# Sparse attention on one core: the attention stream starts one share sooner, and the second tile of an output pair may take the way over DRAM and be turned one product later

## The chip, the cores and the metric

The kernel runs on one core of one Trainium2 chip. The metric is device time in microseconds (us), the median of several executions. All arithmetic is fp32 except where stated.

## The reference

```python
# x: (2708, 1024); adj: (2708, 2708), 0/1, each entry is 1 with chance 0.0014771; W_*: (1024, 1024)
h = relu(layernorm(x))
q, k, v = h @ W_q.T + b_q, h @ W_k.T + b_k, h @ W_v.T + b_v
z = (q @ k.T) / sqrt(1024) * adj
z = where(z == 0, -10000, z)
out = x + relu(softmax(z, axis=1) @ v)
```

A row of adj has about four ones. Softmax over such a row is a sum over its few neighbours, so the kernel never forms the 2708 x 2708 scores.

## The kernel before

**Stages.** The kernel reads adj once, lists each row's neighbours, and sorts the rows by their number of neighbours into 21 full tiles of 128 rows (tiles 0 to 20) and a rest of 20 rows. Tile t has a fixed number K[t] of neighbour slots. W_q and W_k are multiplied into one matrix M, so that a score is a dot product of a row q = h M with a neighbour's row of h. The values are not formed per neighbour: the attention weights add up neighbours' rows of h into a row u, and only u is multiplied by W_v.

**TensorE: units.** The matrix products are written as 20 units (`units`), each of 256 rows, a pair of tiles, against a 1024 x 1024 matrix: units 0 to 9 make q from h (pairs (0,1), (2,3), ...), units 10 to 19 make the output from u. The output pairs are, in order, (6,5) (4,3) (2,0) (20,7) (13,17) (18,12) (19,11) (15,10) (14,1) (16,9); the 21st tile, 8, is left over (`alone`) and done singly at the end, its turned rows being `T_alone`. A unit is a Strassen-like scheme of seven products (`multiply`), each eight matmuls of 128x512, in the order s2, a12, s4, s3, then a11 and s1 of the next unit (`between`, `opened`), then a22. A `psy` row is a product by a matrix in wlow (the differences T), a `ps` row one by M.

**Operands.** A product needs its rows turned, with the 1024 columns across the partitions. `blocks` makes the operands of a pair: `upper` makes a11 and a12 from the pair's first tile, `lower` makes a22 and, by four additions, s1 to s4 from its second tile. While unit n runs, `after(i)` is called after its i-th product; the upper half of unit n+1 is written at i == 0 and the lower half at i == 2. A tile of u gets there in one of two ways:
- held in SBUF and turned by TensorE: eight transposes of 128x128 (L415) into two PSUM tiles pt, of which ScalarE copies one (L718) and VectorE reads the other in its additions (L722);
- faced: ScalarE copies u into v in another order (L944), a DMA of ScalarE's queue writes v to u_dram (L946), `load_rows` reads it back by quarters into `or` with four DMAs of SyncE's queue (L700), and VectorE turns it by two stream transposes (L705). In the four additions one becomes a subtraction in place.

`sums` decides at the end of a tile's sums: it is faced if that end falls, in program order, no later than product 2 of the unit two ahead of the one that uses it. `load_rows` of unit n+2 is called in unit n at i == 4; before it the stream is driven on until both tiles are done.

**Attention.** One Python generator, `attention`, goes over the tiles in the order 6, 5, 4, 3, 2, the second half of the hosts (SECOND), 0, 20, 7, 13, 17, 18, 12, 19, 11, 15, 10, 14, 1, 16, 9, 8. For a tile it gathers the rows of q (`fetch`, tile pq, L612) and the neighbours' rows of h into buffers g0 to g10 and two buffers in wlow (L610), both as indirect DMAs from POOL's queue. VectorE makes one dot product per slot (L863), ScalarE the exponentials (L872), VectorE the weights (L906 to L911), ScalarE the first term of u (L912), VectorE the other terms (L923). A buffer g goes back to the gathers when its sum is done. While a tile's sums run, the next tile's scores may run ahead of its weights. VectorE's order is the program's order, and all engines work through theirs in order. `advance(share)` lets the generator emit about three us of VectorE's work after each product, beginning in unit 5 (FIRST is 4); the share is 20.9/7 or, near the end, 21.5/7 us, less 2.3/7 for each faced tile of the next pair. VectorE's other work stands between these: the evictions of the products (L1130, the u2 of a unit's c12) and the operands.

Of the kernel before, what the change touches and what calls it, by code (L numbers as in the profile page):

```python
# [30 lines left out]
BARE = 20  # L31
# [34 lines left out]
def tile_preln_masked_attention(  # L66
# [109 lines left out]
    t = 0  # L176
    while t < NT:
# [4 lines left out]
        t = e  # L182
# [28 lines left out]
    def row_tile(name):  # L211
        return work.tile([P, D], FT, tag="row", name=name, bufs=ROWS)
# [402 lines left out]
    FIRST = EARLY // 2  # L615
# [187 lines left out]
    wanted, g_of, tq, first_q = [], {}, {}, []  # L803
# [11 lines left out]
    def ask(t):  # L815

        g_of[t] = []
        wanted.extend((t, s) for s in range(K[t]))

    def fetch(t):  # L820

        if t not in g_of:
            ask(t)
        if t == BARE:
            return
        assert formed.issuperset(range(EARLY) if t < EARLY or t == SECOND else (t,)), t
        tq[t] = work.tile([P, D], FT, tag="hT", name=f"pq_{t}", bufs=2)
        if t == SECOND:
            assert EARLY in formed
            gather(tq[t][:HP], q_dram[:, :], t, SLOTS - WIDE, HP)  # L830
            nc.gpsimd.dma_start(tq[t][HP:], q_late[:HP, :])
        elif t >= EARLY:
            nc.gpsimd.dma_start(tq[t], q_late[(t - EARLY) * P:(t - EARLY + 1) * P, :])
        else:
            got = gather(tq[t], q_dram[:, :], t, SLOTS, P)
            if t == order[0]:
                first_q.append(got)

    def fill():
        while wanted and free:  # L840
            t, s = wanted.pop(0)
            g = free.pop(0)
            if s == K[t]:
                half = slice(HOSTS.index(t) * HP, (HOSTS.index(t) + 1) * HP)
                nc.gpsimd.dma_start(g[:HP], v_dram[half, :])
            else:
                with tc.issue_after(first_q[0].ins) if first_q else nullcontext():
                    gathered.append(gather(g, h_dram[:, :], t, s, P, skip=True))
            g_of[t].append(g)

    def chained(step):

        with tc.issue_after(chain[-1].ins):
            chain.append(step())
# [64 lines left out]
    def sums(t):  # L919
        u, coef, m = us.pop(t)  # L920
        for s in range(0 if t in EMPTY else 1, K[t]):
            fill()
            chained(lambda: nc.vector.scalar_tensor_tensor(  # L923
                u, g_of[t][s], coef[:, s:s + 1], u, op0=ALU.mult, op1=ALU.add))
            free.append(g_of[t][s])
            yield 1.3
        fill()
        if t in HOSTS:
            chained(lambda: nc.vector.scalar_tensor_tensor(
                u[:HP], g_of[t][K[t]][:HP], m[:HP, 3:4], u[:HP], op0=ALU.mult, op1=ALU.add))  # L930
            free.append(g_of[t][K[t]])
            yield 1.3
            fill()
        g_of.pop(t)
        if t == SECOND:
            nc.sync.dma_start(v_dram, u)
            whole_second.append(True)
            return
        unit = next((n for n, pair in enumerate(units) if pair[0] == "o" and t in pair[1:]), len(units))
        if now <= [unit - 2, 2] or unit >= len(units) - 1:  # L940
            faced_tiles.add(t)
        if t in faced_tiles:
            v = row_tile(f"v_{t}")
            nc.scalar.copy(v.rearrange("p (a c r) -> p c a r", a=QUADS, r=QP),  # L944
                           u.rearrange("p (c a r) -> p c a r", a=QUADS, r=QP))
            nc.scalar.dma_start(u_dram[t * P:(t + 1) * P, :], v)  # L946
        elif near(t):
            held[t] = u
        else:
            nc.sync.dma_start(u_dram[t * P:(t + 1) * P, :], u)  # L950
        done.add(t)
# [7 lines left out]
    def attention(order):  # L959
        for t in order[:2]:  # L960
            ask(t)
        free.extend(slots)

        fetch(order[0])
        fill()
        yield 0.0
        marked(0, EARLY)
        yield 0.0
        after = order[1:] + [None, None]
        yield from scores(order[0], after[0])  # L970
        for i, t in enumerate(order):
            nxt = after[i]
            ahead = nxt is not None and K[t] + K[nxt] <= HIGH + 1
            part = scores(nxt, after[i + 1]) if nxt is not None else iter(())
            if ahead:

                for _ in range(min(2, K[nxt] - 1)):
                    yield next(part, 0.0)
            weights(t)
            yield 0.6  # L980
            if ahead:
                yield from part
            yield from sums(t)
            yield from part
# [4 lines left out]
    order = [6, 5, 4, 3, 2, 0, 20, 7, 13, 17, 18, 12, 19, 11, 15, 10, 14, 1, 16, 9, 8]  # L989
# [3 lines left out]
    spent, now = [0.0], [0, 0]  # L993
# [5 lines left out]
    def advance(us):  # L999

        spent[0] -= us
        while spent[0] < 0:
            step = next(stream, None)
            if step is None:
                break
            spent[0] += step
# [192 lines left out]
    o_pairs = [(order[i], order[i + 1]) for i in range(0, FULL - 1, 2)]  # L1199
    alone = order[-1]  # L1200
    units = [("q",) + p for p in q_pairs] + [("o",) + p for p in o_pairs]
# [29 lines left out]
        summed.append(True)  # L1231

    single = {}

    opened(0)
    for n, unit in enumerate(units):
# [6 lines left out]
        turn = n in (0, FIRST - 1)  # L1243
        share = (20.9 if n < len(units) - 5 else 21.5) / 7
        if n in (last_q, last_q + 1):
            share -= 2.3 / 7 * (n - last_q + 1)
        nxt = units[n + 1] if n + 1 < len(units) else None
# [4 lines left out]
        def after(i):  # L1252
# [43 lines left out]
                nc.vector.tensor_scalar(msq, msq, MLIMIT, None, op0=ALU.is_gt)  # L1296
            if n > FIRST:
                advance(share)
            if nxt is not None:

                if i == (3 if n == 0 else 4 if turn else 0):
                    ops_of[n + 1] = blocks(*rows_of[n + 1], nc.gpsimd if n + 1 < FIRST - 1 else None)
                    with tc.issue_after(products[-1].ins) if n + 1 == FIRST else nullcontext():
                        ops_of[n + 1][1]()
                if i == (4 if n == 0 else 5 if turn else 2):
                    ops_of[n + 1][2]()
                    rows_of.pop(n + 1)
                    if n == last_q - 1:
                        all_rows()
                if i == 3:  # L1310
                    banks_of[n + 1] = banks_for(bp_sb)
                if i == 6 and n + 2 < FIRST:
                    natural_rows(n + 2)
                if i == (2 if FIRST <= n <= last_q - 2 else 3 if n == last_q else 4) and n + 2 > FIRST and n + 2 < len(units) and n + 2 not in rows_of:
                    while units[n + 2][0] == "o" and not done.issuperset(units[n + 2][1:]):
                        advance(1.0)
                    rows_of[n + 2] = load_rows(units[n + 2])
# [259 lines left out]
```

## Time and profile before

| | |
|---|---|
| median of 3 runs | 627.59 us (627.45 to 627.91) |
| profiled execution | 628.18 us, its span 626.5 us |
| mean granted TensorE clock | 0.999 |
| TensorE busy | 619.6 us, 99% of the span |
| VectorE | 525.1 us, 84% |
| ScalarE | 291.1 us, 46% |
| GpSimd (POOL) | 366.2 us, 58% |
| DMA packets | 182.19 MB, mean 291 GB/s |

Times of single instructions are from the profiled execution, in us from the start of its span; its own time is 0.59 us above the median. PE is TensorE, PEld its weight loads, DVE VectorE, ACT ScalarE, SP SyncE. A row of a timeline has the start, the duration, the engine, the line of the kernel, the operation, what is written and read, and the shapes; a bracket at its end is the idle time of the engine just before, with what ended it. A row of grouped instructions has their count, then busy time and the mean in ns, then idle time ahead of them and what ended most of it.

### The profile page before, as it was taken

How to read it: one execution, taken by the hardware profiler on the slowest of the kernel's cores; microseconds unless marked ns; L12 is line 12 of the kernel's file. 1: busy time of each engine (PE TensorE's matmuls, PEld its weight loads, DVE VectorE, ACT ScalarE, POOL GpSimd, SP SyncE). 2: the span in 40 equal slices, each digit the busy share in tenths (PEclk: the TensorE clock that was granted, in tenths of full speed). 3: DMA queues.
4: the chain of work that ended last, by engine and by line, in shares of the span. 5: the costliest groups of instructions: out<-in, count | busy, mean ns of one | idle time of the engine just before them, and what ended most of it. 6: DMA issues, size and time to landing. Idle time of an engine off the chain costs nothing.

```text
span 626.5 us, 6070 instructions
## 1 busy us (share of the span) xinstructions
PE 619.6 (99%) x1579; PEld 310.9 (50%) x1579; DVE 525.1 (84%) x1022; ACT 291.1 (46%) x421; POOL 366.2 (58%) x394
## 2 busy tenths in 40 slices
PE   9999999999999999999999999999999999999996
PEld 5777767444444445454444444444444444444442
DVE  4999878987988845989897999998997998988741
ACT  3538985759677373344232433444342334342300
POOL 2648870786668477666543333778465776752241
PEclk9999999999999999999999999999999999999999
DMA  8999898688697559996687999999999999996481
GB/s 338 407 360 328 336 349 324 211 272 326 237 377 271 175 180 360 322 410 197 198 348 203 394 313 272 316 346 346 333 270 351 296 312 301 335 280 167 104 298 71
DMA packets 65088, 182.19 MB, mean 291 GB/s; under 512 B 9959, under 2 KB 20023, under 8 KB 64408
## 3 DMA queue, kind: packets, MB, share of 16 engines
q0 software_dynamic: 26656, 86.02, 43.3%
q1 hardware_dynamic: 31594, 71.53, 33.5%
q10 hardware_dynamic: 6798, 24.20, 9.8%
q8 instruction: 14, 0.23, 0.2%
q14 instruction: 26, 0.21, 0.1%
HBM read 146.70 MB, written 43.36 MB: 303 GB/s over the span
## 4 chain that ended last, share of the span: by engine, by line
PE 99%; POOL 0%; DVE 0%; POOLq 0%; issue 0%
PE ps L1010 46%; PE psy L1010 33%; PE ps_y L476 7%; PE ps_x L476 4%; PE ps_z L476 4%; PE pt L415 3%; PE ps_y L511 1%; PE ps_h L1229 0%; PE ps_v L594 0%; DVE y_alone L1393 0%; POOL out_dram L1377 0%; POOLq L1399 0%; POOL hsum L121 0%; PE ps_in L678 0%; PE ps_all L680 0%
## 5 line engine op out<-in xcount | busy, mean ns | idle before, releaser
L610 POOL DMA_INDIRECT g<-h_dram,tab x92 | 114.0, 1239 | 58.9 <-DVE u L923 18.5
L1010 PE MATMUL ps<-M,a 128*128 128x512 f32 x320 | 144.0, 593 | 0.0
L1010 PE MATMUL psy<-wlow,s 128*128 128x512 f32 x320 | 143.9, 592 | 0.0
L863 DVE SCALAR_TENSOR_TENSOR junk<-g,pq 128x1024 uint8<-128x1024 f32 x91 | 111.1, 1221 | 7.3 <-DMA g<-h_dram,tab 3.1
L1010 PE MATMUL ps<-M,s 128*128 128x512 f32 x240 | 107.9, 592 | 0.0
L1010 PEld LDWEIGHTS psy<-wlow,s 128*128 128x128 f32 x320 | 60.0, 190 | 72.1 <-issue 71.4
L1010 PEld LDWEIGHTS ps<-M,a 128*128 128x128 f32 x320 | 59.9, 190 | 71.8 <-issue 71.4
L923 DVE SCALAR_TENSOR_TENSOR u<-g,coef,u 128x1024 f32<-128x1024 f32 x68 | 87.1, 1281 | 3.9 <-ACT u L912 2.4
L389 DVE FIND_INDEX8 at<-ones,adj 128x8 uint32<-128x685 f32 (+1 forms) x88 | 74.5, 866 | 0.0
L1010 PEld LDWEIGHTS ps<-M,s 128*128 128x128 f32 x240 | 45.5, 190 | 57.2 <-issue 56.5
L1010 PE MATMUL psy<-wlow,a 128*128 128x512 f32 x160 | 71.9, 592 | 0.0
L368 ACT ACTIVATE sized<-adj 128x2708 uint8<-128x2708 f32 (+1 forms) x22 | 54.2, 2466 | 6.8 <-DMA adj<-in_adj_dram 5.5
L1114 POOL DMA_INDIRECT y<-in_x_dram,tab x19 | 35.3, 1856 | 32.2 <-ACT y L1131 18.9
L298 POOL TENSOR_TENSOR hsum<-hsum,x 128x256 f32<-128x256 f32 (+1 forms) x56 | 38.7, 734 | 26.1 <-DVE wlow L444 22.0
L1010 PEld LDWEIGHTS psy<-wlow,a 128*128 128x128 f32 x160 | 30.4, 190 | 38.3 <-issue 36.6
L808 POOL DMA_INDIRECT out_dram<-y,tab x21 | 25.8, 1229 | 21.7 <-issue 13.9
L1010 PE MATMUL ps<-wlow,s 128*128 128x512 f32 x80 | 36.0, 593 | 0.0
L944 ACT COPY v<-u 128x1024 f32<-128x1024 f32 x19 | 19.9, 1045 | 26.4 <-DVE u L923 23.1
L912 ACT ACTIVATE u<-g,coef 128x1024 f32<-128x1024 f32 x17 | 19.5, 1149 | 23.0 <-DVE coef L911 17.8
L626 POOL DMA_INDIRECT tab_dram<-tab,pos_i x22 | 21.6, 982 | 14.7 <-DVE pos_i L689 9.2
L760 ACT COPY ps<-bp_sb 128x512 f32<-128x512 f32 x42 | 24.5, 594 | 10.3 <-DVE y L1149 9.6
L276 ACT ACTIVATE x<-x,r 128x1024 f32<-128x1024 f32 (+1 forms) x22 | 25.8, 1232 | 6.3 <-POOL r L266 6.3
(253 smaller groups left out, 849.7 us busy)
## 6 DMA issues: line engine op xcount, KB each, us to landing
adj<-in_adj_dram SPq DMA_DIRECT2D x21, 1354.0 KB, 9.6
x<-in_x_dram SPq DMA_DIRECT2D x21, 512.0 KB, 4.3
h_dram<-x ACTq DMA_DIRECT2D x21, 512.0 KB, 8.0
u_dram<-v ACTq DMA_DIRECT2D x19, 512.0 KB, 6.7
or<-u_dram SPq DMA_DIRECT2D x76, 128.0 KB, 6.9
q_late<-q SPq DMA_DIRECT2D x12, 512.0 KB, 5.4
pq<-q_late POOLq DMA_DIRECT2D x12, 512.0 KB, 9.3
M<-in_wv_dram SPq DMA_DIRECT2D x3, 1024.0 KB, 10.1
```

Source lines behind the costliest of these rows:

```text
L276: nc.scalar.activation(xs[i][:n], xs[i][:n], AF.Relu, bias=r[:n, 4, i:i + 1], scale=r[:n, 3, i:i + 1])
L298: small.append(nc.gpsimd.tensor_add(hsum[:n, cols], hsum[:n, cols], xt[:n, cols]))
L368: nc.scalar.activation(sized[:n], a[:n, :, :PW], AF.Abs, accum_out=total[:n, t:t + 1])
L389: nc.vector.max_index(at[:n, k - first_k, g, :], ones[:n, 0:8], a[:n, g, :])
L476: mm = nc.tensor.matmul(bank, a_tile(o + H * a[0], a[1], i), b(o), start=first and o == 0, stop=(o == H - 1), skip_group_check=True)
L610: return nc.gpsimd.indirect_dma_start(out=dst, out_offset=None, in_=src, in_offset=off, bounds_check=N - 1, oob_is_err=False)
L760: nc.scalar.copy(return_[h], row[:, h * NB:(h + 1) * NB])
L808: to = nc.gpsimd.indirect_dma_start(out=out, out_offset=bass.IndirectOffsetOnAxis(ap=ptab.bitcast(U32)[:n, t, SLOTS:SLOTS + 1], axis=0), i ...
L863: chained(lambda: nc.vector.scalar_tensor_tensor(junk, g_of[t][s], 1.0, tq[t], op0=ALU.mult, op1=ALU.mult, accum_out=zall[:, t, s:s + 1]))
L923: chained(lambda: nc.vector.scalar_tensor_tensor(u, g_of[t][s], coef[:, s:s + 1], u, op0=ALU.mult, op1=ALU.add))
L1010: mm = nc.tensor.matmul(bank, a[:, c, :], b[:, c, :], start=False, stop=(c == 3), skip_group_check=True)
L1114: return nc.gpsimd.indirect_dma_start(out=y[:n], out_offset=None, in_=x, in_offset=off, compute_op=ALU.add)
```

## The change

```diff
--- before.py
+++ after.py
@@ -821,7 +821,7 @@
 
         if t not in g_of:
             ask(t)
-        if t == BARE:
+        if t == BARE or t in tq:
             return
         assert formed.issuperset(range(EARLY) if t < EARLY or t == SECOND else (t,)), t
         tq[t] = work.tile([P, D], FT, tag="hT", name=f"pq_{t}", bufs=2)
@@ -937,7 +937,7 @@
             whole_second.append(True)
             return
         unit = next((n for n, pair in enumerate(units) if pair[0] == "o" and t in pair[1:]), len(units))
-        if now <= [unit - 2, 2] or unit >= len(units) - 1:
+        if now <= [unit - 2, 4 if unit < len(units) and t == units[unit][2] else 2] or unit >= len(units) - 1:
             faced_tiles.add(t)
         if t in faced_tiles:
             v = row_tile(f"v_{t}")
@@ -962,6 +962,7 @@
         free.extend(slots)
 
         fetch(order[0])
+        fetch(order[1])
         fill()
         yield 0.0
         marked(0, EARLY)
@@ -1231,6 +1232,7 @@
         summed.append(True)
 
     single = {}
+    late_unit = ("o",) + o_pairs[8]
 
     opened(0)
     for n, unit in enumerate(units):
@@ -1296,13 +1298,15 @@
                 nc.vector.tensor_scalar(msq, msq, MLIMIT, None, op0=ALU.is_gt)
             if n > FIRST:
                 advance(share)
+            elif (n, i) == (FIRST, 6):
+                advance(share)
             if nxt is not None:
 
                 if i == (3 if n == 0 else 4 if turn else 0):
                     ops_of[n + 1] = blocks(*rows_of[n + 1], nc.gpsimd if n + 1 < FIRST - 1 else None)
                     with tc.issue_after(products[-1].ins) if n + 1 == FIRST else nullcontext():
                         ops_of[n + 1][1]()
-                if i == (4 if n == 0 else 5 if turn else 2):
+                if i == (4 if n == 0 else 5 if turn else 3 if nxt == late_unit else 2):
                     ops_of[n + 1][2]()
                     rows_of.pop(n + 1)
                     if n == last_q - 1:
```

Four things change.
- `fetch(order[1])` stands right behind `fetch(order[0])`, ahead of the first `fill()`, so the rows of q for the first two tiles, 6 and 5, are gathered before any neighbour's row. `fetch` returns at once when it meets a tile a second time.
- `advance(share)` is called once more, after product 6 of unit 4 (FIRST). Everything in the stream moves ahead by one share, as far as the forced driving in `load_rows` leaves it there.
- The second tile of an output pair is faced when its sums end by product 4, not 2, of the unit two ahead. Two tiles meet this anew, 10 (second of unit 17) and 1 (second of unit 18). The shares of units 16 and 17 fall by 2.3/7 us for it.
- `late_unit` is unit 18, the pair (14, 1): its lower half is written in unit 17 at i == 3, one product later.

What this does to the order of TensorE, in unit 16, where the operands of unit 17 are made; u_10 is tile 10's rows, ps0 and ps1 and psy are the banks of unit 16. Before:

```order
L1010 MATMUL psy_3108<-wlow_170,a22_3026 128x512 x4
L1010 MATMUL psy_3238<-wlow_170,s2_3182 128x512 x4
L415 MATMUL pt_3299<-ident_75,u_10_3123 128x128 x4
L415 MATMUL pt_3306<-ident_75,u_10_3123 128x128 x4
L1010 MATMUL ps0_3194<-M_147,a12_3153 128x512 x4
L1010 MATMUL ps1_3196<-M_147,s4_3184 128x512 x4
```

and now:

```order
L1011 MATMUL psy_3117<-wlow_170,a22_3045 128x512 x4
L1011 MATMUL psy_3250<-wlow_170,s2_3190 128x512 x4
L1011 MATMUL ps0_3208<-M_147,a12_3161 128x512 x4
L1011 MATMUL ps1_3210<-M_147,s4_3192 128x512 x4
L1011 MATMUL psy_3250<-wlow_170,s3_3185 128x512 x4
L1011 MATMUL ps0_3350<-M_147,a11_3286 128x512 x4
```

The eight transposes of u_10 are gone. The same is so for u_1 in unit 17, and nothing else on TensorE changes its place.

VectorE in unit 17, where the operands of unit 18 are made; u_9 is the sum of tile 9, or_1 tile 1's rows read back, a11, a12, a22 and s1 to s4 the operands, u2 the eviction of unit 17's second product (L1130 before, L1131 now). Before:

```order
L923 SCALAR_TENSOR_TENSOR u_16_3388<-g2_1427,coef_3387,u_16_3388 128x1024
L906 SCALAR_TENSOR_TENSOR w_9_3442,m_9_3461<-w_9_3442,keys_93 128x7
L910 RECIPROCAL m_9_3461<-m_9_3461 128x1
L911 TENSOR_SCALAR coef_3462<-w_9_3442,m_9_3461 128x7
L923 SCALAR_TENSOR_TENSOR u_9_3463<-wlow_170,coef_3462,u_9_3463 128x1024
L722 TENSOR_TENSOR s1_3484<-a22_3477,pt_3479 128x512
L722 TENSOR_TENSOR s3_3486<-a11_3420,pt_3479 128x512
L722 TENSOR_TENSOR s2_3488<-s1_3484,a11_3420 128x512
L722 TENSOR_TENSOR s4_3490<-a12_3422,s2_3488 128x512
L923 SCALAR_TENSOR_TENSOR u_9_3463<-wlow_170,coef_3462,u_9_3463 128x1024
L923 SCALAR_TENSOR_TENSOR u_9_3463<-g5_1430,coef_3462,u_9_3463 128x1024
L1130 TENSOR_TENSOR u2_3453<-ps1_3345,u2_3453 128x512
```

and now:

```order
L906 SCALAR_TENSOR_TENSOR w_9_3449,m_9_3468<-w_9_3449,keys_93 128x7
L910 RECIPROCAL m_9_3468<-m_9_3468 128x1
L911 TENSOR_SCALAR coef_3469<-w_9_3449,m_9_3468 128x7
L923 SCALAR_TENSOR_TENSOR u_9_3470<-g5_1430,coef_3469,u_9_3470 128x1024
L923 SCALAR_TENSOR_TENSOR u_9_3470<-wlow_170,coef_3469,u_9_3470 128x1024
L705 STREAM_TRANSPOSE a22_3488<-or_1_3376 128x4x4x32
L705 STREAM_TRANSPOSE s3_3490<-or_1_3376 128x4x4x32
L722 TENSOR_TENSOR s1_3492<-a22_3488,s3_3490 128x512
L742 TENSOR_TENSOR s3_3490<-a11_3427,s3_3490 128x512
L722 TENSOR_TENSOR s2_3495<-s1_3492,a11_3427 128x512
L722 TENSOR_TENSOR s4_3497<-a12_3429,s2_3495 128x512
L1131 TENSOR_TENSOR u2_3456<-ps1_3352,u2_3456 128x512
```

The additions stand behind two sums of tile 9 where it was one, with a pair of stream transposes ahead of them, and right ahead of u2 where two sums stood between. In unit 16 the order changes likewise for tile 10: a pair of stream transposes (of or_10) comes ahead of the additions, which stay at i == 2.

POOL's queue at the start of attention; pq_6 and pq_5 are rows of q, g0 to g5 neighbours' rows of h, tab the table of indices. Before:

```order
L612 DMA pq_6_1611<-q_dram_64,tab_97 128x1024
L610 DMA g0_1425<-h_dram_63,tab_97 128x1024
L610 DMA g1_1426<-h_dram_63,tab_97 128x1024
L610 DMA g2_1427<-h_dram_63,tab_97 128x1024
L610 DMA g3_1428<-h_dram_63,tab_97 128x1024
L610 DMA g4_1429<-h_dram_63,tab_97 128x1024
L610 DMA g5_1430<-h_dram_63,tab_97 128x1024
L612 DMA pq_5_1673<-q_dram_64,tab_97 128x1024
```

and now:

```order
L612 DMA pq_6_1611<-q_dram_64,tab_97 128x1024
L612 DMA pq_5_1613<-q_dram_64,tab_97 128x1024
L610 DMA g0_1425<-h_dram_63,tab_97 128x1024
L610 DMA g1_1426<-h_dram_63,tab_97 128x1024
L610 DMA g2_1427<-h_dram_63,tab_97 128x1024
L610 DMA g3_1428<-h_dram_63,tab_97 128x1024
L610 DMA g4_1429<-h_dram_63,tab_97 128x1024
L610 DMA g5_1430<-h_dram_63,tab_97 128x1024
```

The gather of pq_5 has moved ahead of six gathers of h. Elsewhere, ScalarE loses two copies of a22 (L718) and gains the copies v_10 and v_1 with their writes, which come behind ScalarE's last eviction of unit 14 and its copy of unit 16's s3 product; SyncE gains eight issues, four quarters each for or_10 and or_1.

## The prediction, made before the changed kernel was run

> **What bounds the kernel.** I read the page first (busy times, then the chain that ended last), then TensorE's timeline, then VectorE's and TensorE's rows at the end.
>
> ```profile
> PE 619.6 (99%) x1579; PEld 310.9 (50%) x1579; DVE 525.1 (84%) x1022; ACT 291.1 (46%) x421; POOL 366.2 (58%) x394
> ...
> PE 99%; POOL 0%; DVE 0%; POOLq 0%; issue 0%
> PE ps L1010 46%; PE psy L1010 33%; PE ps_y L476 7%; PE ps_x L476 4%; PE ps_z L476 4%; PE pt L415 3%; PE ps_y L511 1%; PE ps_h L1229 0%; PE ps_v L594 0%; DVE y_alone L1393 0%; POOL out_dram L1377 0%; POOLq L1399 0%; POOL hsum L121 0%; PE ps_in L678 0%; PE ps_all L680 0%
> ```
>
> TensorE is busy for 99% of the span and is 99% of the chain. The time is therefore the sum of TensorE's own instructions as long as no operand comes late. So two questions decide: what TensorE no longer does, and which operand then comes last. The transposes of rows of u (pt from u, L415) are on that chain:
>
> ```profile
> L415 PE MATMUL pt<-ident,u x16: 272/272/273, 519.1 to 544.8; 128*128 128x128 f32 x16
> ```
>
> ```profile
> 515.66 3.60 PE L1010 MATMUL psy<-wlow,s 128*128 128x512 f32 x8
> 519.10 1.04 PE L415 MATMUL pt<-ident,u 128*128 128x128 f32 x8
> 519.97 3.60 PE L1010 MATMUL ps<-M,a 128*128 128x512 f32 x8
> 523.40 3.60 PE L1010 MATMUL ps<-M,s 128*128 128x512 f32 x8
> ...
> 544.00 1.04 PE L415 MATMUL pt<-ident,u 128*128 128x128 f32 x8
> 544.88 3.60 PE L1010 MATMUL ps<-M,a 128*128 128x512 f32 x8
> ...
> 558.61 3.60 PE L1010 MATMUL ps<-M,s 128*128 128x512 f32 x8
> ...
> 603.25 3.60 PE L1010 MATMUL ps<-M,T_alone 128*128 128x512 f32 x8
> ```
>
> The first column is the start in us. A product starts 3.43 us after the one ahead of it (519.97 to 523.40); no row shows an idle time. The eight transposes of tile 10 put off the next product by 519.97 - 519.10 = 0.87 us, those of tile 1 by 0.88 us.
>
> **The transposes that go.** In the changed order both groups are gone from TensorE and nothing else there moves: 0.87 + 0.88 = 1.75 us less on the chain. Each transpose is listed with 272 ns, but eight of them overlap to 0.87 us, so the spacing is the price. The Trainium skill, TensorE: Matmul & The Clock Gate, Part 4 on PE-mode transposes, gives about 275 ns for one in a kernel, mostly read latency. By that, taken as time held, 16 would give 4.4 us; the trace agrees with the duration (272 ns) and not with its use as a spacing.
>
> **What VectorE takes over.** Tiles 10 and 1 now come back from DRAM by quarters and are turned by VectorE: for each a pair of stream transposes, while the four additions stay as many. ScalarE loses the copy of a22 and gains the copy v (L944).
>
> ```profile
> L863 DVE SCALAR_TENSOR_TENSOR junk<-g,pq 128x1024 uint8<-128x1024 f32 x91 | 111.1, 1221 | 7.3 <-DMA g<-h_dram,tab 3.1
> L923 DVE SCALAR_TENSOR_TENSOR u<-g,coef,u 128x1024 f32<-128x1024 f32 x68 | 87.1, 1281 | 3.9 <-ACT u L912 2.4
> ...
> L944 ACT COPY v<-u 128x1024 f32<-128x1024 f32 x19 | 19.9, 1045 | 26.4 <-DVE u L923 23.1
> ```
>
> ```profile
> 495.16 0.70 DVE L705 STREAM_TRANSPOSE a<-or 128x512 f32<-128x512 f32 x1
> 495.79 0.67 DVE L705 STREAM_TRANSPOSE s<-or 128x512 f32<-128x512 f32 x1
> ...
> 502.20 0.69 DVE L1130 TENSOR_TENSOR u<-ps,u 128x512 f32<-128x512 f32 x1 [0.48 <-PE ps L1010]
> ...
> 521.51 1.29 DVE L722 TENSOR_TENSOR s<-a,pt 128x512 f32<-128x512 f32 x2 [1.69 <-ACT a L718]
> ...
> 527.04 0.69 DVE L1130 TENSOR_TENSOR u<-ps,u 128x512 f32<-128x512 f32 x1 [0.57 <-PE ps L1010]
> ...
> 550.80 1.28 DVE L722 TENSOR_TENSOR s<-a,pt 128x512 f32<-128x512 f32 x2
> ...
> 588.55 1.28 DVE L929 SCALAR_TENSOR_TENSOR u<-wlow,m,u 64x1024 f32<-64x1024 f32 x1
> ...
> 601.50 1.25 DVE L705 STREAM_TRANSPOSE T_alone<-or 128x1024 f32<-128x1024 f32 x1 [10.60 <-DMA or<-u_dram]
> ```
>
> A pair is 0.70 + 0.67 = 1.37 us. VectorE keeps its order, so the pairs put off what stands behind them, down to the last sum of tile 8 (588.55, ends 589.8). From there its rows go out and come in and are turned at 601.50, and TensorE takes them next:
>
> ```profile
> 602.82 0.19 PEld L1010 LDWEIGHTS ps<-M,T_alone 128*128 128x128 f32 x1 [0.24 <-DVE T_alone L705]
> ```
>
> T_alone ends at 602.75 and its first weights load at 602.82: 0.07 us to spare. This is what is late next. TensorE gains the whole 1.75 us only if the last sum ends 1.75 - 0.07 = 1.68 us sooner, by 588.1.
>
> Does it? I count VectorE's order between two evictions of u2 (L1130), scores (L863) at 1.22 us and sums (L923) at 1.28 us. From unit 15's (502.20) to unit 16's (527.04) there are 9 scores and 4 sums before, 7, 6 and one pair after: -2.44 + 2.56 + 1.37 = +1.49 us. The wait of 1.69 us for ScalarE's a goes, since no pt is read there, and the 0.57 us for TensorE can be used up: 24.84 + 1.49 - 1.69 - 0.57 = 24.07 us, so 526.3. TensorE itself releases it no sooner than 523.40 - 0.87 + 3.43 = 526.0. From there to the last sum there are 16 scores and 17 sums before, 15, 15 and one pair after: -1.22 - 2.56 + 1.37 = -2.4 us, of 62.7 us. The last sum then ends at 526.3 + 60.3 = 586.6, with 1.5 us to spare. The earlier start pays for this: attention is some 3 operations ahead at unit 16 and spends the lead on the two pairs. How much of it holds is the unknown term. At best T_alone costs nothing; at worst the order in unit 15, with one more group of weights and sums that wait for ScalarE's u, begins the row later by 1.6 us (the longest such wait, below), and the last sum ends at 588.2, on the edge. I take no cost, since both ends lie within 0.1 us of it.
>
> **The turn one product later.** The additions for unit 18 stood at 550.80; now the pair and they come at 526.3 + 23.8 - 1.28 (one sum less ahead) = 548.8. Then s1 is ready at 548.8 + 1.37 + 0.69 = 550.9, and TensorE wants it at 558.61 - 1.75 = 556.9. Cost nothing, 6 us of cover. Unit 17's have more: they stand at 521.5, and their s1 is first used after 533.
>
> **The added transfers.** Two writes and two reads of 512 KB, on queues that are full.
>
> ```profile
> 520.00:530.00 10.00, 10.00 (x26) 4.50 (x25) 7.85 (x10) 3.50 (x6) 5.86 (x6) 1.00 0.99 308
> ```
>
> ```profile
> DVE u L923 <- ACT u L912: 2.8, 2, 1.6
> DVE s L722 <- ACT a L718: 1.7, 1, 1.7
> DVE u L1130 <- PE ps L1010: 1.1, 2, 0.6
> DVE p L1126 <- ACT taken L1080: 0.6, 1, 0.6
> DVE w L906 <- ACT w L872: 0.3, 1, 0.3
> ```
>
> The first row is a stretch of 10 us: engines, clock (1.00), DMA share 0.99, 308 GB/s. 2.1 MB at 308 GB/s is 6.8 us of all transfer engines between some 495 and 548. The second view is all of VectorE's waits from 500 to 590: none is for a DMA, so gathers have room. I take no cost, and up to 1.7 us (one 512 KB transfer at that rate) as the other end. Here a rule speaks against the change. The Trainium skill, DMA: Bandwidth & Descriptors, Queues, rings and completion order, says that each engine takes its queues in turn, packet by packet, so the new rows share with every gather under way. The share of 0.99 agrees; by the rule the late end is the likelier one, the sum 1.7 - 1.5 = 0.2 us worse.
>
> Tile 1's rows are the tight ones. Landing times of writes and reads of u_dram, minimum, median and maximum, for 480 to 560 and, of the reads, over the run:
>
> ```profile
> DMA to landing us min/median/max: 5.7/6.5/7.9
> ```
>
> ```profile
> DMA to landing us min/median/max: 4.9/6.9/16.3
> ```
>
> The three last sums end at 526.3 + 0.6 + 3.8 = 530.7, v 1.05 later at 531.8, written by 538.3, four issues of 0.43 us (1.7), read by 546.5. VectorE comes there at 548.8: 2.3 us of cover.
>
> **The start.** One gather of q moves ahead of six gathers of h on POOL's queue.
>
> ```profile
> 228.50 0.99 POOL L612 DMA_INDIRECT pq<-q_dram,tab  x1 [1.42 <-DMA tab<-tab_dram]
> ```
>
> ```profile
> 236.52 1.23 DVE L863 SCALAR_TENSOR_TENSOR junk<-g,pq 128x1024 uint8<-128x1024 f32 x1 [1.30 <-DMA g<-h_dram,tab]
> ...
> 243.43 1.22 DVE L863 SCALAR_TENSOR_TENSOR junk<-g,pq 128x1024 uint8<-128x1024 f32 x1 [2.83 <-issue]
> ...
> 250.83 1.29 DVE L722 TENSOR_TENSOR s<-a,pt 128x512 f32<-128x512 f32 x2 [1.79 <-ACT a L718]
> ```
>
> ```profile
> 261.49 3.60 PE L1010 MATMUL ps<-wlow,s 128*128 128x512 f32 x8
> ```
>
> The first score waits some 1.3 us longer (one issue with its gap), the fourth no longer 2.83 us, since its q is there. The additions of L722 wait for ScalarE anyway, and TensorE wants s1 only at 261.49, over 9 us after s1 is made at 251.5. Neither end touches TensorE. Of the rows gathered for the next units, moved back by a place or two on POOL, none is turned for 15 us.
>
> **Sum.** -1.75 + 0 = -1.75 us. The profiled execution took 628.18 us for its span of 626.5, 0.59 above the median of the runs, 627.59: it should take 626.4, and the median 627.59 - 1.75 = 625.85, say 625.9.
>
> **Rivals.**
> 1. T_alone takes the transposes' place. If the last sum ends 0.5 us or more after 588.1, TensorE waits for it and the time is 625.9 plus that: at 589.8, its place before, the gain is 0.07 us and the time 627.5. For it: 0.07 us of room before, 2.7 us of new work on VectorE, full transfer queues. Against: the count above, 1.5 us to spare.
> 2. Slower. Tile 1's rows land late and VectorE stands in front of their transpose with everything behind it. It decides once they land later than 548.8 + 1.5 + 1.8 = 552.1: from there T_alone comes later than before. With the run's longest reading, 16.3 us, they land at 556.3; the last sum ends at 586.6 + 7.5 = 594.1, 6.0 after 588.1, and the time is 631.9. Against: near that place the longest landing is 7.9 us, which gives 549.3.
> 3. A transpose holds TensorE for the whole of its duration: 16 x 0.272 = 4.35 us go, 623.2. The rows at 519.10 and 519.97 speak against it. The page on TensorE named above would read so.
>
> **How the numbers follow.** Forecast 0.62 (T_alone costs under 0.5 us); rival 1 0.27, rival 2 0.09, rival 3 0.02. A measurement tells about 0.2% from no change, 1.26 us: 626.3 and 628.8 are the bounds. The forecast and rival 3 are faster, 0.64; rival 1, from 626.4 to some 628.8, is the same, 0.27; rival 2 slower, 0.09. The range: low 625.4, the forecast less 0.45, the width of the runs shown (627.45 to 627.91); high 627.3, which takes in rival 1 up to a wait of 1.4 us and leaves out its end and rival 2, some 0.15, and rival 3.
>
> **What the next profile would show.** Right: no pt from u; TensorE still 99%, about 1.75 us less busy; T_alone's transpose at or before 599.8 on VectorE; L722's wait for a gone at 521; no wait of L705 for or but the last. Wrong: a gap on TensorE ahead of the product with T_alone (rival 1), or VectorE waiting for or near 549 (rival 2). The sum is wrong if TensorE shows a gap that stands nowhere above, most likely ahead of an s1 or a psy of units 16 to 18.

## The result, and the profile after

The change made the kernel slower, by 0.8%: median 633.89 us of 17 executions (627.48 to 638.01) against 627.86 of 17 of the kernel before (627.45 to 629.06), ratio 1.0082, 95% interval 1.0066 to 1.0097. The ratio compares fast executions alone, so it is not the quotient of the two medians, 1.0096. It is rival 2, with tile 1's rows late. The profiled execution took 631.62 us, 2.3 us under the median, so the trace shows a mild case. The loss varies: two of the 17 executions took 627.48 and 628.87 us.

The page of the changed kernel, busy times and the chain by engine:

```profile
PE 617.9 (98%) x1563; PEld 308.6 (49%) x1563; DVE 527.3 (84%) x1026; ACT 291.2 (46%) x421; POOL 369.8 (59%) x394
...
PE 74%; DMA 12%; DVE 8%; issue 3%; ACT 1%; POOL 1%; SPq 1%; POOLq 0%; DVEq 0%; ACTq 0%
```

TensorE does 1.7 us less, as forecast, but the chain that was 99% TensorE now runs 12% through transfers. TensorE's timeline says where (start, duration, and in brackets the wait ahead):

```profile
515.23 3.60 PE L1011 MATMUL psy<-wlow,s 128*128 128x512 f32 x8
518.67 3.60 PE L1011 MATMUL ps<-M,a 128*128 128x512 f32 x8
...
542.70 3.60 PE L1011 MATMUL ps<-M,a 128*128 128x512 f32 x8
...
556.92 3.67 PE L1011 MATMUL ps<-M,s 128*128 128x512 f32 x8 [0.33 <-DVE s L722]
...
583.28 3.67 PE L1011 MATMUL ps<-M,s 128*128 128x512 f32 x8 [1.73 <-DVE s L722]
...
606.49 3.70 PE L1011 MATMUL ps<-M,T_alone 128*128 128x512 f32 x8 [2.36 <-DVE T_alone L705]
```

At 515 TensorE was 0.43 us ahead of the trace before (515.66). It had been so since 20 us, long before the part that the change touches. At 542.70 it is 2.18 ahead (544.88 before): 1.75 us for the two groups of transposes, to the hundredth. Then three waits follow, 4.42 us together, all for VectorE, and the product with T_alone starts 3.24 us later than before (603.25). From 2.18 ahead to 3.24 behind is 5.42 us; the 1.0 us beyond the waits lies in the gaps around them and in the products behind them, 3.67 to 3.70 us in place of 3.60.

VectorE, in the same execution:

```profile
526.16 0.69 DVE L1131 TENSOR_TENSOR u<-ps,u 128x512 f32<-128x512 f32 x1 [0.22 <-issue]
...
554.74 0.71 DVE L705 STREAM_TRANSPOSE a<-or 128x512 f32<-128x512 f32 x1 [6.07 <-DMA or<-u_dram]
...
592.72 1.28 DVE L929 SCALAR_TENSOR_TENSOR u<-wlow,m,u 64x1024 f32<-64x1024 f32 x1
...
605.19 1.25 DVE L705 STREAM_TRANSPOSE T_alone<-or 128x1024 f32<-128x1024 f32 x1 [10.12 <-DMA or<-u_dram]
```

VectorE stood at tile 1's transposes at 548.67 and waited 6.07 us for the rows. The last sum of tile 8 ended at 594.0, T_alone's rows followed 11.2 us behind it (11.7 before). The two transfers of tile 1's rows, from the chain in order of time (start, duration):

```profile
531.79 7.45 DMA u_dram<-v
540.71 13.91 DMA or<-u_dram
```

The write took 7.45 us, 1.0 more than the forecast 6.5; the read 13.9, twice the forecast 6.9. Transfers issued from 530 to 560 us, the kernel before and then the changed one (count, for some the size, median time from issue to landing at the end):

```profile
or<-u_dram SPq DMA_DIRECT2D x4, 128.0 KB, 7.1
...
g<-h_dram,tab POOLq DMA_INDIRECT x9, 7.6
y<-in_x_dram,tab POOLq DMA_INDIRECT x3, 8.7
```

```profile
or<-u_dram SPq DMA_DIRECT2D x8, 128.0 KB, 13.2
...
g<-h_dram,tab POOLq DMA_INDIRECT x8, 13.1
y<-in_x_dram,tab POOLq DMA_INDIRECT x2, 12.5
```

It is not tile 1's rows alone: the medians of other transfers in that stretch grow too, gathers of h by 5.5 us and of y by 3.8. The transfer engines had no free time in either kernel. From 540 to 550 us, before and then changed (the last three numbers are TensorE's granted clock, the transfer engines' share of busy time and GB/s):

```profile
540.00:550.00 10.00, 10.00 (x30) 4.82 (x29) 8.21 (x17) 4.99 (x8) 7.80 (x6) 1.00 1.04 342
```

```profile
540.00:550.00 10.00, 10.00 (x25) 4.37 (x24) 6.92 (x11) 4.73 (x8) 8.14 (x6) 1.00 1.06 289
```

### The profile page after: what moved, and what is told of

The parts are those of the page before. It is cut to its first block, busy times and chain, and to the rows that moved or that the text cites. A ratio compares the mean times of both kernels' runs of the same rounds, so it can differ in the third digit from the quotient of the medians.

```text
span 629.8 us, 6066 instructions
## 1 busy us (share of the span) xinstructions
PE 617.9 (98%) x1563; PEld 308.6 (49%) x1563; DVE 527.3 (84%) x1026; ACT 291.2 (46%) x421; POOL 369.8 (59%) x394
## 4 chain that ended last, share of the span: by engine, by line
PE 74%; DMA 12%; DVE 8%; issue 3%; ACT 1%; POOL 1%; SPq 1%; POOLq 0%; DVEq 0%; ACTq 0%
PE ps L1011 33%; PE psy L1011 22%; PE ps_y L476 7%; PE ps_x L476 4%; PE ps_z L476 4%; DMA or<-u_dram 4%; DVE u L923 3%; DMA u_dram<-v 3%; PE pt L415 3%; DMA out_dram<-y,tab 2%; DVE junk L863 2%; DMA y<-tail_dram 1%; DVE s L722 1%; DMA wlow<-in_wq_dram 1%; DVE a L705 1%
## 5 line engine op out<-in xcount | busy, mean ns | idle before, releaser
L610 POOL DMA_INDIRECT g<-h_dram,tab x93 | 122.3, 1315 | 61.7 <-issue 20.0
L923 DVE SCALAR_TENSOR_TENSOR u<-g,coef,u 128x1024 f32<-128x1024 f32 x70 | 89.7, 1282 | 7.7 <-ACT u L912 5.6
L1115 POOL DMA_INDIRECT y<-in_x_dram,tab x19 | 33.7, 1773 | 39.6 <-ACT y L1132 29.2
L808 POOL DMA_INDIRECT out_dram<-y,tab x21 | 27.9, 1328 | 16.3 <-issue 12.8
L944 ACT COPY v<-u 128x1024 f32<-128x1024 f32 x21 | 22.0, 1046 | 31.2 <-DVE u L923 27.7
```

Of the source, the lines that this page charges most:

```text
L610: return nc.gpsimd.indirect_dma_start(out=dst, out_offset=None, in_=src, in_offset=off, bounds_check=N - 1, oob_is_err=False)
L808: to = nc.gpsimd.indirect_dma_start(out=out, out_offset=bass.IndirectOffsetOnAxis(ap=ptab.bitcast(U32)[:n, t, SLOTS:SLOTS + 1], axis=0), i ...
L923: chained(lambda: nc.vector.scalar_tensor_tensor(u, g_of[t][s], coef[:, s:s + 1], u, op0=ALU.mult, op1=ALU.add))
L1115: return nc.gpsimd.indirect_dma_start(out=y[:n], out_offset=None, in_=x, in_offset=off, compute_op=ALU.add)
```

## The experiments

The letters e, f, g, h, k stand for groups of kernels in the order in which they ran; the text takes them by question. Each group ran on one chip, beside the kernel before, 4 to 12 executions of each kernel, and the groups on different chips: before took 631.35, 630.45, 628.13, 630.47 and 628.09 us (e, f, g, h, k). On the chips of e, f and h, TensorE waits 1.2 to 2.3 us near 202 us for unit 4's rows, in the kernel before too (f2). So ratios are compared, and times of a trace only within a group. Theory A: the transfer engines are full, added transfers queue up, tile 1's rows have the closest due time and come late, and VectorE stands in front of them with all that is behind. Rival B: tile 1's own way over DRAM is too long, whatever else is under way. Rival C: the earlier start is itself the harm.

**Is it the start?** g1 keeps the earlier start alone. With that start tile 10 meets the old rule too, so both tiles are held by name.

```diff
-        if now <= [unit - 2, 4 if unit < len(units) and t == units[unit][2] else 2] or unit >= len(units) - 1:
+        if (now <= [unit - 2, 2] and t not in (10, 1)) or unit >= len(units) - 1:
...
-                if i == (4 if n == 0 else 5 if turn else 3 if nxt == late_unit else 2):
+                if i == (4 if n == 0 else 5 if turn else 2):
```

> Only the start of the change: rows of q for two tiles gathered first and attention one share sooner; tiles 10 and 1 both stay held and are turned by TensorE. Theory A (the slowdown is all in tile 1's rows, late behind the added transfers): 0.999 to 1.002 of before, no row of u waited for. Rival C (the earlier start is itself a harm, its gathers stand ahead of other transfers): over 1.003.

Measured 0.9994 (0.9985 to 1.0003), as A gave. In its trace T_alone is early:

```profile
584.36 1.28 DVE L929 SCALAR_TENSOR_TENSOR u<-wlow,m,u 64x1024 f32<-64x1024 f32 x1
597.22 1.25 DVE L705 STREAM_TRANSPOSE T_alone<-or 128x1024 f32<-128x1024 f32 x1 [10.53 <-DMA or<-u_dram]
```

Before, the last sum began at 588.55: the start moves it 4.2 us ahead. It is no harm; it gives the room that the rest spends. Rival C falls. g4 is the changed kernel without the extra share:

```diff
             if n > FIRST:
                 advance(share)
-            elif (n, i) == (FIRST, 6):
-                advance(share)
```

> The changed kernel without the earlier share; tiles 10 and 1 still go over DRAM. A: the stream is up to one share behind, so tile 1's sums end later or at the same place and its rows land no sooner: 1.007 to 1.013. Rival C (the earlier start puts gathers ahead of tile 1's rows): under 1.004, with a wait of VectorE for tile 1's rows of under 2 us.

Measured 1.0215 (1.0192 to 1.0237), worse than either expected: v of tile 1 is written from 536.76 (531.79 with the share), the rows are read from 544.5, and TensorE waits 3.4 us for unit 18's s1 and 5.7 us for T_alone. Part of the excess is clock: the two products behind these waits took 6.52 and 5.42 us in place of 3.60 (last section).

**Is it the traffic?** g2 adds to g1 the transfers without their use.

```diff
             held[t] = u
+            if t in (10, 1):
+                nc.scalar.dma_start(u_dram[t * P:(t + 1) * P, :], u)
...
                 rows.append(held.pop(t))
+                if t in (10, 1):
+                    by_quarters(row_tile(f"unused_{t}"), u_dram[t * P:(t + 1) * P, :])
                 continue
```

> The same as the start alone, with the transfers of the change and without their use: rows of u of tiles 10 and 1 are written to DRAM and read back by quarters into a buffer that nothing reads; TensorE still turns both tiles, and VectorE turns neither. A: level with the start alone, within 0.002, since other transfers have room and nothing waits for these. Rival (the added traffic slows the gathers, and VectorE or TensorE waits for those): 1.004 or more above the start alone.

Measured 1.0038 (1.0020 to 1.0056) against g1's 0.9994 on the same chip, 1.0044 of g1. A's "level" did not hold; the size is the rival's, but its wait for gathers is not in the trace. Gathers issued from 530 to 560, g1 and then g2 with the unused read:

```profile
g<-h_dram,tab POOLq DMA_INDIRECT x7, 7.0
```

```profile
unused<-u_dram SPq DMA_DIRECT2D x4, 128.0 KB, 11.1
...
g<-h_dram,tab POOLq DMA_INDIRECT x8, 12.9
```

The added transfers alone put 5.9 us on the gathers and 4.0 on y (8.5 to 12.5), with nothing else changed. And they cost, though nothing reads them: VectorE does not wait for gathers, as the rival had it, but for the next rows of u, those of tile 16, and T_alone is 5.4 us later than in g1, on the edge again:

```profile
570.96 1.30 DVE L705 STREAM_TRANSPOSE a<-or 128x512 f32<-128x512 f32 x2 [4.14 <-DMA or<-u_dram]
...
602.65 1.25 DVE L705 STREAM_TRANSPOSE T_alone<-or 128x1024 f32<-128x1024 f32 x1 [10.41 <-DMA or<-u_dram]
```

This shows the delay, and not the whole price. Of the 1.8 us by which g2's profiled execution is longer than g1's, TensorE lost some 0.4 at T_alone; most of the rest was there by 372 us, ahead of the added transfers. Where the medians' 2.6 us go was not seen.

f1 and f2 are the changed kernel and the kernel before once more.

> The changed kernel once more, beside the kernel before on the same chip and with the other kernels of this group. Theory A (added transfers queue up ahead of tile 1's rows; VectorE stands in front of them with all that is behind): the stream transpose of tile 1's rows waits 2 to 8 us, the time is 1.003 to 1.010 of before, and it varies from execution to execution by the landing. If it is level with before here, the slowdown belongs to single executions or chips.

> The kernel before, for a trace on the same chip: no wait of VectorE for rows of tiles 10 and 1, T_alone on the edge. Theory A: gathers issued between 530 and 552 us are in flight some 5 us less than in the changed kernel. An extra wait ahead of the transposes of unit 4's rows at 202 us, as in the first group's traces, would show that this wait is the chip's and not the change's.

f1 measured 1.0091 (1.0072 to 1.0110), the slowdown on another chip. Its transpose:

```profile
557.52 0.71 DVE L705 STREAM_TRANSPOSE a<-or 128x512 f32<-128x512 f32 x1 [5.95 <-DMA or<-u_dram]
```

f2's trace has the wait near 202 us (1.6) and no wait of VectorE for rows of tiles 10 and 1; it does not tell landing times, so the 5 us were not compared there.

e2 sends tile 1 alone over DRAM. e3 takes other transfers away: it leaves out the addition of x to tiles 18 and 12 and the writing of their output rows, so its output is not complete.

```diff
# e2
-        if now <= [unit - 2, 4 if unit < len(units) and t == units[unit][2] else 2] or unit >= len(units) - 1:
+        if (now <= [unit - 2, 4 if unit < len(units) and t == units[unit][2] else 2] and t != 10) or unit >= len(units) - 1:
# e3
         while due and due[0][:2] <= tuple(now):
             y, t = due.pop(0)[2:]
+            if t in (18, 12):
+                continue
```

> Tile 10 stays held and is turned by TensorE; tile 1 goes over DRAM and is turned one product later. A: about 1 MB less is queued ahead of tile 1's rows, so they land some 3.4 us sooner than the 554.6 us of the changed kernel's profile, near 551; VectorE waits 2 to 3 us for them, and the time is 627 to 629.5 us. B: they land as late as in the changed kernel and the time is over 633 us.

> The changed kernel without the addition of x to tiles 18 and 12 and without the writing of their output rows: four transfers of 512 KB less between some 510 and 545 us, all else in place. A: tile 1's rows land by 549, VectorE waits under 1 us for them, 626 us. B: they land after 552 and the time stays over 631 us.

In the traces of e2, e3 and f1 VectorE reaches tile 1's transposes at the same time, 551.3 to 551.6 (f1: 557.52 - 5.95), so these three can be set side by side:

```profile
551.59 0.71 DVE L705 STREAM_TRANSPOSE a<-or 128x512 f32<-128x512 f32 x1 [0.18 <-DMA or<-u_dram]
```

```profile
551.30 0.70 DVE L705 STREAM_TRANSPOSE a<-or 128x512 f32<-128x512 f32 x1
```

In e2 (first row) the rows land at the moment they are wanted, in e3 (second) ahead of it, both some 6 us sooner than in f1. Not all of this is traffic: the write of v was issued at 533.44 in e2, 534.50 in e3 and 534.69 in f1. So some 4.7 us are left for the 1 MB that e2 takes away, 3.4 us of all transfer engines at the prediction's rate, and, with a landing at 551.0, 6.2 us for the 2.1 MB of e3, 6.8 us at that rate. B, by which other transfers do not matter, falls as far as these traces go. The times: e2 1.0020 (1.0000 to 1.0041), inside what A gave, and short of a gain with one group of transposes less. e3 1.0035 (1.0007 to 1.0063), not the 626 expected. Its trace is of its fastest execution (629.55 of 629.55 to 638.06) and shows T_alone 0.6 us late; what the slower ones waited for was not seen.

**Does VectorE stand in front?** g3 undoes the turn one product later, f3 turns one more product later.

```diff
-                if i == (4 if n == 0 else 5 if turn else 3 if nxt == late_unit else 2):
# g3
+                if i == (4 if n == 0 else 5 if turn else 2):
# f3
+                if i == (4 if n == 0 else 5 if turn else 4 if nxt == late_unit else 2):
```

> The changed kernel with the lower half of unit 18 at i == 2 as before, that is without the turn one product later. A (tile 1's rows land when they land, and all that stands behind their transposes on VectorE waits with them): VectorE comes to the transposes 2.6 us sooner, two sums of tile 9 more stand behind the wait, T_alone comes 2.6 us later, 1.012 to 1.014 of before. Rival (s1 of unit 18 alone sets the end): as the changed kernel, 1.009.

> The changed kernel with unit 18's lower half written one more product later (i == 4): two sums and the eviction of u2 stand ahead of tile 1's transposes now, 3.2 us of VectorE's work. A: VectorE fills 3.2 us of its wait with work that was behind it, so T_alone comes up to 3.2 us sooner, and the time is 2 to 3 us under the changed kernel on the same chip; TensorE still waits for s1 of unit 18, 0.3 us or as much as tile 1's rows are late. Rival (the harm is at T_alone or s1 by TensorE's own order, not by what stands behind the wait on VectorE): no change against the changed kernel, or slower by s1.

g3: 1.0128 (1.0112 to 1.0144), in A's range; f3: 1.0033 (1.0014 to 1.0053) against f1's 1.0091 on the same chip, 3.7 us less, more than the 2 to 3 that A gave. The waits at the transposes, g3 and then f3:

```profile
554.65 0.71 DVE L705 STREAM_TRANSPOSE a<-or 128x512 f32<-128x512 f32 x1 [10.45 <-DMA or<-u_dram]
```

```profile
557.45 0.71 DVE L705 STREAM_TRANSPOSE a<-or 128x512 f32<-128x512 f32 x1 [1.55 <-DMA or<-u_dram]
```

The rows land at the same moment (554.6 in g3 and the trace after; 557.4 in f3 and f1). What changes is only how much of VectorE's work is behind the wait: 10.45 us of waiting with more behind it, 5.95, and 1.55 with two sums and an eviction ahead. That is the price list of a transpose's place, and the turn at i == 3 in the change saves about 0.4% against i == 2 (g3 and f1, ratios from two chips).

**Half of the change.** e1 and h3 are one kernel: the start, tile 10 over DRAM, tile 1 held.

```diff
-        if now <= [unit - 2, 4 if unit < len(units) and t == units[unit][2] else 2] or unit >= len(units) - 1:
+        if (now <= [unit - 2, 4 if unit < len(units) and t == units[unit][2] else 2] and t != 1) or unit >= len(units) - 1:
...
-                if i == (4 if n == 0 else 5 if turn else 3 if nxt == late_unit else 2):
+                if i == (4 if n == 0 else 5 if turn else 2):
```

> The start of the change is kept; tile 10 goes over DRAM, tile 1 stays held and is turned by TensorE at its old place. Theory A (backlog: the transfer engines are full from 480 to 560 us, so what is added is added to the queue ahead of every later transfer, and tile 1's rows, the only ones with a close due time, land late): no tile 1 rows, so no late rows; one group of transposes (0.87 us) goes, 626.7 us. Rival B (tile 1's own way over DRAM is too long whatever else is under way): the same, 626.7. Rival C (the earlier start of attention puts more gathers into the queue and is itself the harm): over 628, with VectorE or TensorE waiting for gathers or for T_alone.

> The start with tile 10 alone over DRAM, measured again: 0.9986 (627.0 against 627.86), one group of transposes less and nothing late. Rival (T_alone or a row of the next unit takes half of it): 0.9993 to 1.000.

0.9987 (0.9970 to 1.0004) and 0.9996 (0.9978 to 1.0013). C's "over 628" is 1.0002, at the upper end of both intervals; no row of tile 10 is waited for, and g1 has settled C. Whether all of 0.87 us remains, 0.9986, neither settles.

**The rows in time.** e4 moves tile 1's rows from v within SBUF, f4 those of tiles 10, 1 and 8.

```diff
+    def by_blocks(dst, v, queues):
+        faced.append(dst)
+        for a in range(QUADS):
+            for g in range(QUADS):
+                eng = queues[(a * QUADS + g) % len(queues)]
+                eng.dma_start(dst[a * QP:(a + 1) * QP, g * D // QUADS:(g + 1) * D // QUADS],
+                              v[g * QP:(g + 1) * QP, a * D // QUADS:(a + 1) * D // QUADS])
...
-            nc.scalar.dma_start(u_dram[t * P:(t + 1) * P, :], v)
+            if t in (1,):    # f4: (10, 1, 8)
+                direct[t] = v
+            else:
+                nc.scalar.dma_start(u_dram[t * P:(t + 1) * P, :], v)
...
+                if t in direct:
+                    by_blocks(rows[-1], direct.pop(t), (nc.sync, nc.scalar) if t == alone else (nc.sync,))
...
```

> Tile 1's rows go from v to their place in SBUF by 16 DMAs of 32 rows by 1 KB each on SyncE's queue, without the write to DRAM and the read back; tile 10 as in the changed kernel. Half of tile 1's added traffic goes, and one of two passes through the queue. A and B both: the last block is issued at 531.8 + 16 x 0.43 = 538.7 us and lands 7 to 14 us later, 546 to 553; at the early end no wait and 625.9 us, at the late end 629. If the issues cost more than 0.43 us each, later.

> The changed kernel with the rows of tiles 10, 1 and 8 moved within SBUF by 16 DMAs of 32 rows by 1 KB each (tile 8's on two queues), without the write to DRAM and the read back: 2.1 MB of the added 4.2 MB of reads and writes go, and one pass through the queue for each. A: tile 1's rows land by 549, T_alone some 3 us sooner than in the trace with tile 1 alone moved so; TensorE keeps the 1.75 us, 0.997 of before. Rival (sixteen issues on SyncE's queue, 6.9 us, are as slow as what they replace): as with tile 1 alone, 1.000.

e4 1.0002 (0.9982 to 1.0021), f4 1.0009 (0.9992 to 1.0026): the loss is gone, with no wait at the transposes, and no gain comes; f4's 0.997 is out. k1 and k2 are e4 and f4 with f3's edit, the turn at i == 4.

> The changed kernel with tile 1's rows moved within SBUF (16 DMAs of 32 rows by 1 KB) and unit 18's lower half at i == 4. Theory A: the rows land near 551.4 us as in the kernel with that move alone, and VectorE comes at 552, so nothing waits for them, T_alone comes 1.5 us sooner than there: 0.997 to 0.999 of before. Rival (T_alone stays late by what VectorE's own order holds, sums that wait for ScalarE's u): 1.000.

> The same with tiles 10 and 8 moved within SBUF too. A: less traffic ahead of tile 1's rows, 0.997 to 0.999; rival (the issues for tile 8's blocks put off T_alone): 1.000 to 1.002.

k1 0.9999 (0.9984 to 1.0014), k2 1.0001 (0.9992 to 1.0010), the rivals' numbers. In k1's trace nothing of u is late, and yet:

```profile
588.24 1.28 DVE L938 SCALAR_TENSOR_TENSOR u<-wlow,m,u 64x1024 f32<-64x1024 f32 x1
```

```profile
602.82 3.70 PE L1024 MATMUL ps<-M,T_alone 128*128 128x512 f32 x8 [0.87 <-DVE T_alone L714]
```

The last sum begins 0.3 us sooner than before, not the 1.7 that it takes, and TensorE waits 0.87 us for T_alone: rival 1, once rival 2 is out of the way. In k2's trace T_alone is 0.2 us late and VectorE then holds up a22's product by 0.8.

**More lead.** h1 and h2 advance by more at the start; k3 does not, but gives larger shares from unit 10 on and has f3's edit.

```diff
             elif (n, i) == (FIRST, 6):
-                advance(share)
+                advance(2 * share)    # h2: 3 * share
# k3
-        share = (20.9 if n < len(units) - 5 else 21.5) / 7
+        share = (20.9 if n < len(units) // 2 else 21.5) / 7
```

> The changed kernel with attention two shares sooner, not one: both tiles over DRAM, tile 1 turned one product later. A with a due time (the way over DRAM takes some 23 us when the transfer engines are full, so what counts is when tile 1's sums end): leaving the one share out put v of tile 1 5 us later and the time 7 us up; one share more should put it 2 to 4 us sooner, VectorE waits 2 to 4 us for the rows in place of 6, T_alone comes that much sooner: 0.999 to 1.004. Rival (the stream is bounded by its gathers, which the earlier start only puts closer together in the full queues): v ends where it did, as the changed kernel, 1.009.

> The same with three shares. A with a due time: v of tile 1 4 to 7 us sooner than in the changed kernel, no wait or one under 1 us for tile 1's rows, 0.997 to 1.000. Rival (gathers bound the stream): 1.006 to 1.009, with VectorE waiting for neighbours' rows or scores standing ahead of unit 5's operands at the start, TensorE waiting there.

> The changed kernel with the lower half of unit 18 at i == 4, and the share 21.5/7 in place of 20.9/7 from unit 10 on, which gives the stream up to 3 us more lead by unit 15 without a denser start. A with a due time: tile 1's sums end 1 to 3 us sooner than in the kernel with i == 4 alone (1.0033), 0.999 to 1.002. Rival (VectorE is full from 480 us on, so a lead in the order is none in time): 1.003 to 1.005.

h1 1.0091 (1.0063 to 1.0118), h2 1.0142 (1.0117 to 1.0167), k3 1.0018 (0.9999 to 1.0036). h1's time is its rival's, h2's is worse than either expected, k3's lies inside what A gave. In h1's trace VectorE waits for nothing at tile 1's transposes (554.56 us), where A gave a wait of 2 to 4; the time goes elsewhere. VectorE's waits for gathers from 236 to 300 us (in all, how many, the longest), and TensorE behind them:

```profile
DVE junk L863 <- DMA g<-h_dram,tab: 10.1, 3, 3.6
```

```profile
297.01 3.27 PE L1011 MATMUL psy<-wlow,a 128*128 128x512 f32 x7 [2.74 <-DVE q L1097]
```

Scores that are issued before their gathers have landed stand ahead of an eviction that TensorE needs. So the lead that the start can give ends before two shares. With the lead in the middle (k3) there is no wait at tile 1's transposes, and T_alone is 1.2 us late.

No version is clearly faster than before.

## Why the prediction was wrong, point by point

- **The transposes that go**: right, 1.75 us, 0.87 and 0.88. Rival 3 (4.35 us) is out.
- **VectorE up to tile 1**: right, closer than its terms. The eviction of u2 was forecast at 526.3 and came at 526.16; VectorE was forecast at tile 1's transposes at 548.8 and stood there at 548.67. The counts of scores and sums were right, and the wait for ScalarE's a (1.69) was gone. But the row began 0.6 us later, with the eviction of unit 15 at 502.80 for 502.20, and took 23.36 us for the forecast 24.07; that the two cancel is luck.
- **The added transfers**: the step that failed. "I take no cost, and up to 1.7 us (one 512 KB transfer at that rate) as the other end" was the wrong size. The prediction had the share, 0.99, and the sum, 6.8 us of all transfer engines, and then took tile 1's landing from the trace before, 6.9, as if it stayed. With no free time on the transfer engines, those 6.8 us are not hidden: transfers behind them come later. The read took 13.9, 7.0 more; g2 shows 4 to 6 us on gathers and y with the traffic alone. That gathers had room said only that they would not be the ones to wait. The delay is not the same for all: tile 1's write, 1.0 us longer, had little of it. Why the read took nearly all of it stays open.
- **"2.3 us of cover"** at tile 1's rows was the right thing to ask for, and the 7 us more of the read were to be set against it. The sum itself is 0.4 off: 538.3 + 1.7 + 6.9 is 546.9, not 546.5, so 1.9 us. The reason for 0.09 on rival 2, "near that place the longest landing is 7.9 us", came from a trace without the added traffic.
- **The Trainium skill's rule**, DMA: Bandwidth & Descriptors, Queues, rings and completion order (each engine takes its queues in turn), was weighed and priced at 0.2 us. Runs g1 and g2 agree with it as far as they go: beside the new rows the gathers under way take longer to land, 12.9 us for 7.0. The turns themselves no run shows.
- **Rival 2's price**: landing past 552.1 decides, and the rows landed at 554.6. The mechanism was right, the chance was not. It gave a last sum at 594.1 for a landing at 556.3, and 594.0 was measured; that these agree is luck. For a landing at 554.6 the same sum gives 592.4; of the 1.6 us that it lacks the next point explains 1.2.
- **The last sum at 586.6**: without the 6.07 us it would have been 587.9 at best, 0.2 inside the limit, not 1.5. From u2 to the last sum the trace before has 15 scores, not the 16 that I counted, and the trace after has 15 too: one score, 1.22 us, that does not go. (Sums go from 20 to 18, for 17 and 15 in the prediction; the difference is right.) With so little in hand rival 2 decides, by its own sum, at 550.8 and not at 552.1. k1, with rows in time but other transfers and the turn at i == 4, shows what is left: T_alone late, rival 1, and no gain. The forecast of a gain would have failed there too.
- **The turn one product later**, "Cost nothing": it was worth about 0.4% here, since it took work out from behind the wait.
- **The start**, "Neither end touches TensorE": right (g1).

That the median lies 2.3 us over the profiled execution was not traced. The mean clocks of the 17 executions, 0.994 to 1.000, lie under 0.998 in 11 of them; 0.3% is 1.9 us, and the last section shows a way to that. But executions with 0.999 and 1.000 took 632.90, 633.89 and 634.63 us, so the clock is not all of it; the rest stays open.

## What to carry to other kernels

Where the transfer engines' share is 1.0, as here, do not price an added transfer by the landing times of the trace before. Allow for a delay of up to its engine time on what is issued behind it (here 6.8 us by the sum, and 1.0 to 7.0 in the traces), and set that against the closest due time, of other tiles too. In an in-order engine the price of a late operand is what stands behind it; moving the instruction that waits behind ready work is the cheapest cure (3.7 us in f3). And when a critical engine is relieved, check the next edge with the same count twice: here a slack of 0.07 us had to grow by 1.7, and one miscounted score was most of the 1.5 us that seemed to be in hand.

## What the runs showed of the hardware

A wait of TensorE can cost twice. In f3 it waits 1.96 us for T_alone, and the product behind it takes 5.40 us in place of 3.60; in g4 the waits are longer:

```profile
606.47 5.40 PE L1011 MATMUL ps<-M,T_alone 128*128 128x512 f32 x8 [1.96 <-DVE T_alone L705]
```

```profile
559.95 6.52 PE L1011 MATMUL ps<-M,s 128*128 128x512 f32 x8 [3.39 <-DVE s L722]
```

g4's stretch behind that wait (the last three numbers are the granted clock, the DMA share and GB/s):

```profile
560.00:565.00 5.00, 5.00 (x6) 2.10 (x7) 4.86 (x6) 1.12 (x2) 1.54 (x1) 0.50 1.02 159
```

The granted clock was 0.50 in these 5 us, and in f3 0.50 from 608 to 610 us. After the wait of 2.36 us in the changed kernel's own trace the product took 3.70 us, and 3.70 after one of 2.79 us in f1. The Trainium skill, TensorE: Matmul & The Clock Gate, Part 1, puts half clock after an idle window of about 3.4 us whose phase is not the kernel's own. The trace of f3 differs from that length, with half clock after a wait of 1.96 us, and the measurement decides; that half clock follows one wait and not another would fit a phase of its own, which no run here shows. So waits of 2 to 3 us here cost between 0.1 and 1.8 us more, by the execution.
